# Two transformer layers on one core: layer 0's rows projected group by group, even token tiles first, norms on GpSimd, ternary steps moved

## The chip, the cores and the metric

The program runs on one core of one Trainium2 chip. The metric is the device time of one execution in microseconds (us); lower is better. The engines are called by the profile's names: PE (TensorE matmul), PEld (its weight loads), DVE (VectorE), ACT (ScalarE), POOL (GpSimd) and SP (SyncE, which here only issues DMAs).

## The reference

Two layers, each of which normalizes its input over the last axis and adds attention and a feed-forward block to it. x has 2 batches of 1024 tokens of 256 features. All arithmetic is float32 except where the weights are made ternary. Cut to layer 0, which the change touches:

```
xn = layernorm(x)
# attention, 16 heads of 16 features; the reshape takes a head out of the token axis
Q = (xn @ Wq.T).reshape(2, 16, 1024, 16)      # K and V alike
weights = softmax(causal(Q K^T) / sqrt(16))
x1 = x + (weights V) @ Wp.T + bp
# feed-forward with ternary weights, one scale for each 64 weights
h  = relu(xn @ ternary(W_fc).T) ** 2
x1 = x1 + rms_norm(h) @ ternary(W_proj).T
```

The reshape (1024 tokens of 256 features into 16 heads of 1024 positions of 16 features) gives head h the tokens 64h to 64h+63, and each of these tokens gives 16 positions. Layer 1 is a latent attention with 16 heads and a gated feed-forward block with ternary weights; the change leaves its code as it is.

## The kernel before

**Tiles.** x lies in SBUF as x_sb, 16 tiles of 128 tokens, 8 for each batch (E = 256, SC = 512, S = 1024, KC = 2). `ln_stats` takes means and variances of tiles on DVE and a square root on ACT, `ln_rstd` the reciprocal on DVE, `ln_norm` normalizes two tiles into one buffer xn (there is one such buffer), and `ln_turn` transposes these on PE and copies them with ACT into xnT, which holds the normalized tokens of a batch with the features on the partitions.

**Projections.** `project(b, i, m, k)` makes half m of the features of q, k or v (i = 0, 1, 2) for half k of batch b: two matmuls with 512 moving columns. The profile's L228 shows each float32 matmul as two records. When both halves k are there, L246 stores 128 rows of 1024 tokens to DRAM (rows), in an SP DMA. `fetch(g, i)` reads group g's rows back with four SP DMAs (L256), so that the 16 features of a head lie on partitions; group g = 4b + h4 has the four heads h4, h4+4, h4+8, h4+12 of its batch, that is, 64 tokens of each 256. `permute(g, i)` reorders the fetched rows into head tiles (DVE for group 0's k, ACT for group 0's q and group 1's k, else POOL). k and v share one staging buffer.

**The order.** All engines run an order written out by hand (`manual_schedule`). Ahead of the loop stand a prologue (tiles 0 to 7 normalized and turned, k and q of batch 0 projected in full, group 0's k and q fetched and permuted, tiles 8 to 11 turned, one ternary step), and then a loop over groups g = -1 to 8 with 12 steps n each. In a step of group g the row maxima of group g+1 are made (`maxima`: matmuls L307, reductions on DVE L318 and L323), the scores and weights of group g (`scores`: L348, the exponential on ACT at L355, the causal cut on POOL at L358), the product with v of two steps earlier (`product`), and one piece of `fill`, the queue of PE work: the 12 projections of batch 1 first (all in group 0), then layer 0's feed-forward (L430 and L461), from group 1 on. Group -1 has only group 0's maxima, and beside them v of batch 0, the last tiles' norms and turns, and group 1's fetches and permutes.

In group -1 the maxima go through two PSUM pairs (`ps_pair`): a step's first pair waits until DVE has reduced the step before's first pair. From group 0 on they use `ps_bank`, three banks shared with projections, transposes and the feed-forward.

**Ternary steps.** Eight blocks of the feed-forward's weights are made ternary by `ternary`: begin (two ACT passes, L197 and L199), scale (one matmul, L203), pick (five DVE passes, L207 to L215, then two POOL passes, L216 and L217). One stands in the prologue, four in group -1 (n = 2, 3, 10, 11) and three in group 0 (n = 2, 3, 10).

**Buffers.** The projections' SBUF results are in the tag "four" (4 buffers). The tag "temp" (6 buffers, given out in turn) holds the discarded output of the L318 reductions (junk), q_th of the ternary steps and the feed-forward's relu and sq.

Of the kernel before, what the change touches and what calls it, by code (L numbers as in the profile page):

```python
# [17 lines left out]
F32 = mybir.dt.float32  # L18
BF16 = mybir.dt.bfloat16
AF = mybir.ActivationFunctionType  # L20
ALU = mybir.AluOpType
# [25 lines left out]
def two_layers(ctx: ExitStack, tc: tile.TileContext, a: dict, out: bass.AP):  # L47
# [13 lines left out]
    for g in range(4):  # L61
        nc.sync.dma_start(x_sb[:, 4 * g : 4 * g + 4, :], x_d[:, 4 * g : 4 * g + 4, :])
# [41 lines left out]
    with ExitStack() as scope:  # L104
# [48 lines left out]
        def ln_stats(g):  # L153
            for n in range(4 * g, 4 * g + 4):
                st = small.tile([P, 6], F32, tag="ln_st", name="ln_st")
                nc.vector.bn_stats(st, x_sb[:, n, :])
                nc.vector.bn_aggr(mv[:, n, :], st)
            r = rstd[:, 4 * g : 4 * g + 4]
            nc.scalar.activation(r, mv[:, 4 * g : 4 * g + 4, 1], AF.Sqrt, bias=eps["ln"])

        def ln_rstd(g):
            r = rstd[:, 4 * g : 4 * g + 4]
            nc.vector.reciprocal(r, r)

        def ln_norm(n):

            xn = l0t.tile([P, SC], F32, tag="xn", name="xn", bufs=1)
            for k in range(2):
                nc.vector.tensor_scalar(
                    xn[:, k * E : (k + 1) * E], x_sb[:, n + k, :], mv[:, n + k, 0:1],  # L170
                    rstd[:, n + k : n + k + 1], ALU.subtract, ALU.mult,
                )
            return xn

        def ln_turn(xnT, n, xn=None):

            xn = ln_norm(n) if xn is None else xn
            pt = ps_bank()
            for k in range(2):
                for kc in range(KC):  # L180
                    nc.tensor.transpose(
                        pt[:, (2 * kc + k) * P : (2 * kc + k + 1) * P],
                        xn[:, k * E + kc * P : k * E + (kc + 1) * P], ident,
                    )
            at = (n % TB) * P
            nc.scalar.copy(
                xnT[n // TB][:, :, at : at + 2 * P], pt.rearrange("p (c t) -> p c t", c=KC)
            )
# [33 lines left out]
        rows, pend = {}, {}  # L222

        def project(b, i, m, k):

            pw = ps_bank()
            for kc in range(KC):
                nc.tensor.matmul(  # L228
                    pw, wqkv[:, i, kc, m * P : (m + 1) * P],
                    xnT[b][:, kc, k * SC : (k + 1) * SC], start=(kc == 0), stop=(kc == KC - 1),  # L230
                )
            if (b, i, m) not in pend:
                pend[b, i, m] = l0t.tile([P, S], F32, tag="four", name=f"proj{i}_{b}_{m}", bufs=4)
            half = pend[b, i, m][:, k * SC : (k + 1) * SC]
            if b or m:
                nc.scalar.activation(half, pw, AF.Copy, scale=0.25 if i == 0 else 1.0)
            elif i == 0:
                nc.vector.tensor_scalar(half, pw, 0.25, None, ALU.mult)
            else:
                nc.vector.tensor_copy(half, pw)  # L240
            if k == 0:
                return
            proj = pend.pop((b, i, m))
            if m == 0:
                rows[b, i] = dram.tile([2 * P, S], F32, tag=f"rows{b}{i}", name=f"rows{b}{i}")
            nc.sync.dma_start(rows[b, i][m * P : (m + 1) * P, :], proj)  # L246
# [3 lines left out]
        def fetch(g, i):  # L250

            b, h4 = divmod(g, 4)
            src = rows[b, i].rearrange("(j d) t -> d j t", d=D0)
            for c in range(4):
                at = 256 * c + GC * h4
                nc.sync.dma_start(stage[i][32 * c : 32 * c + D0], src[:, :, at : at + GC])  # L256
# [163 lines left out]
        def ffn(n):  # L420
# [56 lines left out]
        fill = [  # L477
            lambda i=i, m=m, k=k: project(1, i, m, k)
            for i in (1, 0, 2) for m in range(2) for k in range(2)
        ] + [x for n in range(B * S // SC) for x in ffn(n)]  # L480
# [236 lines left out]
        with tc.manual_schedule():  # L717

            ln_stats(0)
            ln_rstd(0)  # L720
            ln_turn(xnT, 0)
            ln_turn(xnT, 2)
            project(0, 1, 0, 0)
            project(0, 1, 1, 0)
            ln_stats(1)
            ln_rstd(1)
            ln_turn(xnT, 4)
            ln_turn(xnT, 6)
            for m in range(2):
                project(0, 1, m, 1)  # L730
            fetch(0, 1)
            for m in range(2):
                for k in range(2):
                    project(0, 0, m, k)
            fetch(0, 0)
            begin, scale, pick = weight_steps.pop(0)
            begin()
            ln_stats(2)
            ln_rstd(2)
            ln_turn(xnT, 8)  # L740
            ln_turn(xnT, 10)
            scale()
            permute(0, 1)
            permute(0, 0)
            pick()

            rest = None
            for g in range(-1, NG + 1):
                this, nxt = 0 <= g < NG, g + 1 < NG
                for n in range(12 if g < NG else 2):  # L750
# [4 lines left out]
                    if g < 1 and n in (2, 3, 10, 11) and weight_steps:  # L755
                        block = weight_steps.pop(0)
                        block[0]()
# [25 lines left out]
                    if g == -1:  # L783
                        if n < 2:
                            for k_ in range(2):
                                project(0, 2, n, k_)
                        if n == 1:
                            fetch(0, 2)
                            ln_stats(3)
                            ln_rstd(3)  # L790
                        if n in (4, 6):
                            ln_turn(xnT, 8 + n, xn)
                        if n in (3, 5):
                            xn = ln_norm(12 + n - 3)
                        if n == 4:
                            permute(0, 2)
                            fetch(1, 1)
                            fetch(1, 0)
                        if n in (7, 8):
                            permute(1, 8 - n)  # L800
# [38 lines left out]
                    if g == NG - 3:  # L839
                        if n < 2:  # L840
                            ln_stats(n)
                        if n == 3:
                            ln_rstd(0)
                            ln_rstd(1)
                            xnT1.append(main.tile([P, KC, S], F32, tag="xnT0", name="xnT1_0"))
                        if n in (5, 6, 7, 8):
                            ln_turn(xnT1, 2 * (n - 5), xn)
                        if n in (4, 5, 6, 7):
                            xn = ln_norm(2 * (n - 4))
# [15 lines left out]
            for i in range(TB):  # L865
# [9 lines left out]
                if i == 4:  # L875
                    ln_stats(2)
                if i == 5:
                    ln_rstd(2)
                    xnT1.append(main.tile([P, KC, S], F32, tag="xnT1", name="xnT1_1"))
                    xn = ln_norm(8)  # L880
# [6 lines left out]
            ln_stats(3)  # L887
            ln_rstd(3)
# [411 lines left out]
```

## Time and profile before

| | |
|---|---|
| median of 3 runs | 1390.37 us (1389.55 to 1397.06) |
| the profiled execution | 1391.99 us, span 1390.3 us |
| mean granted PE clock | 0.966 of full |
| PE busy | 1289.6 us (93%), 15614 matmul records |
| DVE, ACT, POOL busy | 765.3 us (55%), 674.3 us (49%), 459.7 us (33%) |
| L228 (projections) in the chain that ended last | 4% |

The chain that ended last is the work followed back from the last instruction to what released it; 81% of it is PE. In the timeline a line gives start, duration (of a merged run of instructions), engine, source line, operation, output<-input, shapes, count, and in brackets the idle time before it and what ended that. The windows of the trace give, for a stretch of time, the busy time of each engine with its count of instructions, then the granted PE clock (1.00 is full), the DMA share and the rate. SPq lines are DMA issues of the SP queue.

### The profile page before, as it was taken

The numbers are of one execution on the slowest core, as the hardware profiler recorded it, in microseconds if no ns is written. First come the engines' busy times: TensorE is split into PE (matmuls) and PEld (weight loads), VectorE is DVE, ScalarE is ACT, GpSimd is POOL, SyncE is SP. The second block draws the span as 40 slices with busy tenths as digits, with TensorE's granted clock in tenths as the row PEclk, the third lists the DMA queues.
The fourth block names the chain that finished last, engine by engine and source line by source line (L and its number), as shares of the span: only waits on it lengthen the run. The fifth ranks groups of instructions, "written<-read, shape, count | busy, mean of one in ns | idle before, by whom it ended". The sixth has DMA issues, their size and how long they took to land.

```text
span 1390.3 us, 36291 instructions
## 1 busy us (share of the span) xinstructions
PE 1289.6 (93%) x15614; PEld 775.9 (56%) x15614; DVE 765.3 (55%) x1909; ACT 674.3 (49%) x1250; POOL 459.7 (33%) x494
## 2 busy tenths in 40 slices
PE   5589999899999998999999789999999999999996
PEld 2233336345355363446577456777766667777665
DVE  3775544546455555313433666666666666666662
ACT  1224474453554744664331555555555555555541
POOL 2133242433422421110321444444444444444420
PEclk9759999989999999999999999999999999999999
DMA  5212120010001000000112400000000000000000
GB/s 190 79 23 69 57 58 16 9 16 8 16 8 16 8 24 0 19 16 1 57 57 85 83 6 18 9 26 7 25 10 25 10 18 17 15 21 10 17 7 21
DMA packets 61008, 41.09 MB, mean 30 GB/s; under 512 B 37648, under 2 KB 56848, under 8 KB 60592
## 3 DMA queue, kind: packets, MB, share of 16 engines
q1 hardware_dynamic: 60000, 35.51, 9.7%
q8 instruction: 122, 2.00, 0.6%
q0 software_dynamic: 416, 2.49, 0.4%
q10 hardware_dynamic: 432, 0.79, 0.2%
q14 instruction: 38, 0.31, 0.1%
HBM read 26.18 MB, written 10.49 MB: 26 GB/s over the span
## 4 chain that ended last, share of the span: by engine, by line
PE 81%; DVE 9%; issue 4%; ACT 4%; POOL 2%; DMA 1%; SPq 0%; DVEq 0%; ACTq 0%; POOLq 0%
PE ps_s L1061 15%; PE ps_m L307 11%; PE ps_o L1109 11%; PE ps_m L558 6%; PE ps_o L373 5%; PE ps_m L461 5%; PE ps_t L1001 4%; PE ps_m L430 4%; PE ps_m L228 4%; PE ps_m L573 3%; PE ps_t L1136 3%; PE ps_t L994 2%; DVE p L1068 2%; DVE pT L1078 1%; PE ps_s L307 1%
## 5 line engine op out<-in xcount | busy, mean ns | idle before, releaser
L1072 ACT ACTIVATE p<-p,nmax 128x1024 f32<-128x1024 f32 (+7 forms) x256 | 197.2, 771 | 209.7 <-DVE nmax L1068 208.9
L1061 PE MATMUL ps_s<-kT,qc 128*128 128x512 f32 (+3 forms) x768 | 279.2, 497 | 20.7 <-DVE nmax L1068 12.0
L1068 DVE CUSTOM_DVE_ANT_0 p<-ps_s,wpe 128x1024 f32<-128x1024 f32 (+7 forms) x256 | 184.8, 744 | 176.3 <-PE ps_s L1061 175.3
L355 ACT ACTIVATE p<-ps_s 128x1024 f32<-128x1024 f32 (+1 forms) x192 | 152.6, 808 | 165.1 <-PE ps_s L348 160.1
L307 PE MATMUL ps_m<-head,head 16*128 16x512 f32 (+3 forms) x672 | 192.5, 547 | 20.7 <-DVE nmx L318 14.0
L1061 PEld LDWEIGHTS ps_s<-kT,qc 128*128 128x128 f32 x768 | 130.6, 190 | 131.4 <-issue 93.5
L1078 DVE STREAM_TRANSPOSE pT<-p 128x1024 f32<-128x1024 f32 (+7 forms) x256 | 185.9, 758 | 22.1 <-ACT p L1072 21.0
L348 PE MATMUL ps_s<-head,head 17*128 17x512 f32 (+3 forms) x768 | 170.7, 549 | 0.0
L1109 PE MATMUL ps_o<-pT,vrep 32*64 32x128 f32 x9216 | 150.6, 273 | 9.8 <-issue 7.2
L1109 PEld LDWEIGHTS ps_o<-pT,vrep 32*64 32x64 f32 x9216 | 133.8, 130 | 37.8 <-issue 30.8
L1034 POOL TENSOR_TENSOR qc<-t,t 32x512 f32<-32x512 f32 x120 | 152.2, 1268 | 8.1
L307 PEld LDWEIGHTS ps_m<-head,head 16*128 16x128 f32 x672 | 71.3, 187 | 120.2 <-DVE nmx L318 37.1
L358 POOL TENSOR_SCALAR_AFFINE_SELECT p<-p 128x256 f32<-128x256 f32 x128 | 51.2, 406 | 240.5 <-ACT p L355 239.2
L1029 POOL TENSOR_TENSOR t<-t,cosq 128x512 f32<-128x512 f32 x28 | 35.7, 1273 | 258.9 <-issue 144.2
L323 DVE TENSOR_REDUCE nmx<-ps_m 128x1 f32<-128x512 f32 x112 | 72.2, 686 | 44.0 <-PE ps_s L348 35.3
L558 PE MATMUL ps_m<-xnT,w 128*128 128x512 f32 x192 | 94.4, 620 | 0.0
L318 DVE CUSTOM_DVE_ANT_0 junk<-ps_m,maskz,nmx 128x512 f32<-128x512 f32 (+3 forms) x112 | 57.7, 548 | 59.6 <-PE ps_s L348 45.1
L373 PE MATMUL ps_o<-p,v 128*32 128x512 f32 (+3 forms) x768 | 82.4, 502 | 0.0
L461 PEld LDWEIGHTS ps_m<-wpr,hT 128*128 128x128 f32 x512 | 61.2, 196 | 17.1 <-issue 6.6
L318 DVE CUSTOM_DVE_ANT_0 junk<-ps_m,maskz 128x512 f32<-128x512 f32 (+3 forms) x112 | 50.5, 487 | 34.3 <-PE ps_s L348 31.6
L461 PE MATMUL ps_m<-wpr,hT 128*128 128x128 f32 x512 | 67.4, 286 | 0.0
L430 PE MATMUL ps_m<-xnT,wfc 128*128 128x512 f32 x128 | 67.1, 649 | 0.2
(176 smaller groups left out, 1758.1 us busy)
## 6 DMA issues: line engine op xcount, KB each, us to landing
rows<-proj SPq DMA_DIRECT2D x12, 512.0 KB, 2.6
stage<-rows SPq DMA_DIRECT2D x96, 64.0 KB, 3.1
w<-in_w SPq DMA_DIRECT2D x3, 768.0 KB, 4.8
x_sb<-in_x SPq DMA_DIRECT2D x4, 512.0 KB, 12.2
x<-x_sb SPq DMA_DIRECT2D x4, 512.0 KB, 3.2
fold_wo<-in_wo SPq DMA_DIRECT2D x8, 256.0 KB, 3.3
vrep<-kv SPq DMA_DIRECT2D x32, 64.0 KB, 2.2
xin<-x SPq DMA_DIRECT2D x16, 128.0 KB, 2.2
```

Of the source, the lines that this page charges most:

```text
L307: nc.tensor.matmul(t[:, :w], quad(q, c, D0)[:, i * P : (i + 1) * P], quad(k, c, D0)[:, k0 : k0 + w], start=True, stop=True, tile_position= ...
L348: nc.tensor.matmul(t[:, c % 2, :w], quad(k, c, D0 + 1)[:, j * P : (j + 1) * P], quad(q, c, D0 + 1)[:, at : at + w], start=True, stop=True, ...
L355: nc.scalar.activation(p[:, pair[0] : pair[0] + 2, :w], t[:, :, :w], AF.Exp)
L373: nc.tensor.matmul(quad(box["o"], c)[:, SC - w :], values[g][:, j, 32 * c : 32 * c + 32], p[:, c, :w], start=(j == 0), stop=(j == 4 * iq + ...
L461: nc.tensor.matmul(po[:, :P], f["h", hc // 2][:, hc % 2, t * P : (t + 1) * P], wpr[:, hc, cols], start=(hc == 0), stop=(hc == NH0 - 1),)
L558: nc.tensor.matmul(pw, w1t[f"w{i + 1}"][:, kc, hc * P : (hc + 1) * P], xnT1[n // 2][:, kc, (n % 2) * SC : (n % 2 + 1) * SC], start=(kc == ...
L1034: (even, odd)[x].tensor_tensor(self.qc[64 + 32 * x : 96 + 32 * x, hh], t1[at : at + 32], t2[at : at + 32], ALU.add,)
L1061: nc.tensor.matmul(sc[:, j * SC + n0 : j * SC + n1], s.q[k].qc[:, h // QP, h % QP, :], kT[:, s.b * S + n0 : s.b * S + n1], start=True, sto ...
L1068: nc.vector.tensor_tensor_reduce(p, sc[:, j * SC : j * SC + w], maskw[:, S - w :], -1.0, 3.0e38, ALU.add, ALU.min, nmax,)
L1072: nc.scalar.activation(p, p, AF.Exp, bias=nmax, scale=-1.0, accum_out=s.rsum[:, k, h : h + 1])
L1078: nc.vector.transpose(s.pT[:, at, h, :], s.p[k, h])
L1109: nc.tensor.matmul(s.o[64 * hh : 64 * hh + 64, c, k * P : (k + 1) * P], vrep[32 * c : 32 * c + 32, s.b * 32 + sb, :], s.pT[32 * c : 32 * c ...
```

## The change

- `project(g, i)` now makes one group's rows: 4 matmuls of 256 moving columns (both halves m of the features; the moving columns are four pieces of 64 tokens), one evacuation of 128x512 (on DVE for k and v of group 0 and v of group 1, else on ACT) into a "temp" buffer, and one store of 256 KB. There are 24 such calls, where there were 24 of two matmuls with a store for each second one.
- x is loaded, and the statistics and the turns are done, by even and odd tiles of each batch. Groups 0 and 1 need the even tiles of batch 0 alone, groups 2 and 3 its odd ones.
- The prologue projects q, k and v of groups 0 and 1 from the even tiles; it takes the statistics of all 16 tiles; it normalizes the odd tiles of batch 0 on POOL.
- Groups 2 and 3 are projected in group -1 (n = 1, 2, 3, 5, 6, 9), and batch 1's tiles are normalized there, on POOL, and turned.
- The eight ternary steps stand in group -1 (n = 8, 10), group 0 (n = 2, 3, 10, 11) and group 1 (n = 2, 3).
- `fill` begins with the 12 calls for groups 4 to 7.

```
-    for g in range(4):
-        nc.sync.dma_start(x_sb[:, 4 * g : 4 * g + 4, :], x_d[:, 4 * g : 4 * g + 4, :])
+    EVEN_ODD = [slice(b * TB + k, (b + 1) * TB, 2) for b in range(B) for k in range(2)]
+    for at in EVEN_ODD:
+        nc.sync.dma_start(x_sb[:, at, :], x_d[:, at, :])
...
-        def project(b, i, m, k):
+        def project(g, i, engine=nc.scalar):
+            b, h4 = divmod(g, 4)
             pw = ps_bank()
+            for m in range(2):
+                for kc in range(KC):
+                    nc.tensor.matmul(
+                        pw[:, m * E : (m + 1) * E], wqkv[:, i, kc, m * P : (m + 1) * P],
+                        xnT[b][:, kc, :].rearrange("p (c h t) -> p c h t", c=4, h=4)[:, :, h4, :],
+                        start=(kc == 0), stop=(kc == KC - 1),
+                    )
+            proj = temp("proj")
...
+            rows[g, i] = dram.tile([2 * P, E], F32, tag=f"rows{g}{i}", name=f"rows{g}{i}")
+            nc.sync.dma_start(
+                rows[g, i].rearrange("(m p) t -> p m t", p=P), proj.rearrange("p (m t) -> p m t", m=2)
+            )
...
+            even, odd, even1, odd1 = EVEN_ODD
+            ln_stats(even)
+            ln_rstd(even)
+            for n in (0, 4):
+                ln_turn(xnT, n, ln_norm(n, 2), 2)
+            project(0, 1, nc.vector)
+            fetch(0, 1)
+            project(0, 0)
+            fetch(0, 0)
+            ln_stats(odd)
+            project(0, 2, nc.vector)
+            project(1, 1)
+            ln_stats(even1)
+            ln_stats(odd1)
+            for at in (odd, even1, odd1):
+                ln_rstd(at)
+            project(1, 0)
+            project(1, 2, nc.vector)
+            for n in (1, 5):
+                ln_turn(xnT, n, ln_norm(n, 2, nc.gpsimd), 2)
+            permute(0, 1)
+            permute(0, 0)
+
+            first = {
+                0: [lambda: turns.append(ln_norm(8, 2, nc.gpsimd))],
+                1: [lambda: fetch(0, 2), lambda: project(2, 1)],
+                2: [lambda: ln_turn(xnT, 8, turns.pop(), 2), lambda: project(2, 0),
+                    lambda: turns.append(ln_norm(12, 2, nc.gpsimd))],
+                3: [lambda: project(2, 2)],
+                4: [lambda: permute(0, 2), lambda: fetch(1, 1), lambda: fetch(1, 0),
+                    lambda: ln_turn(xnT, 12, turns.pop(), 2)],
+                5: [lambda: project(3, 1), lambda: turns.append(ln_norm(9, 2, nc.gpsimd))],
+                6: [lambda: project(3, 0)],
+                7: [lambda: permute(1, 1), lambda: ln_turn(xnT, 9, turns.pop(), 2),
+                    lambda: turns.append(ln_norm(13, 2, nc.gpsimd))],
+                8: [lambda: permute(1, 0)],
+                9: [lambda: project(3, 2), lambda: ln_turn(xnT, 13, turns.pop(), 2)],
+            }
+            turns = []
+            ternary_at = {(-1, 8), (-1, 10), (0, 2), (0, 3), (0, 10), (0, 11), (1, 2), (1, 3)}
...
-                    if g < 1 and n in (2, 3, 10, 11) and weight_steps:
+                    if (g, n) in ternary_at:
```

## The prediction

> **What bounds the kernel now.** I read the page's 40 slices first (34.8 us each; busy tenths), then the start's timeline.
>
> ```profile
> PE   5589999899999998999999789999999999999996
> DVE  3775544546455555313433666666666666666662
> PEclk9759999989999999999999999999999999999999
> ```
>
> From slice 3 on PE is at nine tenths and full clock: time saved ahead of it should last to the end, and PE work or stalls added after it add time. Only the first 100 us have something to give. First the way to the first maximum, SP's queue and then PE and ACT:
>
> ```profile
> 28.07 1.96 SPq L246 DMA_DIRECT2D rows<-proj  x2
> 32.37 1.80 SPq L256 DMA_DIRECT2D stage<-rows  x4
> 34.26 2.63 SPq L246 DMA_DIRECT2D rows<-proj  x2
> 39.24 1.79 SPq L256 DMA_DIRECT2D stage<-rows  x4
> ```
> ```profile
> 13.78 5.12 PE L228 MATMUL ps_m<-xnT,wqkv 128*128 128x512 f32 x8 [0.68 <-ACT xnT L186]
> 43.69 1.95 ACT L265 COPY head<-stage 128x1024 f32<-128x1024 f32 x1 [2.57 <-DMA stage<-rows]
> 45.69 2.09 PE L307 MATMUL ps_s<-head,head 16*128 16x512 f32 x8 [4.97 <-ACT head L265]
> ```
>
> PE is ready to project at 13.8, but k's stores leave at 28, q's fetch at 39, and group -1 starts at 45.7. Then the windows over group -1 (busy time of PE, PEld, DVE, ACT, POOL; clock; DMA):
>
> ```profile
> 50.00:60.00 10.00, 9.00 (x37) 3.46 (x35) 7.52 (x30) 2.47 (x5) 0.00 (x0) 0.96 0.24 99
> 60.00:70.00 10.00, 4.58 (x19) 2.07 (x21) 9.65 (x23) 1.85 (x3) 3.84 (x4) 0.55 0.13 34
> 70.00:80.00 10.00, 9.80 (x32) 3.88 (x32) 7.22 (x13) 2.40 (x2) 3.07 (x2) 0.50 0.35 52
> 90.00:100.00 10.00, 7.86 (x30) 3.14 (x28) 9.22 (x29) 4.15 (x5) 2.53 (x2) 0.50 0.00 1
> ```
>
> DVE leads, behind it PE at half clock, each waiting for the other. PE finds group 0's first banks at 95.8, but DVE reduces into group 0 only after a ternary block:
>
> ```profile
> 96.26 0.68 DVE L207 TENSOR_SCALAR q_sc<-ps_m 128x512 bf16<-128x512 f32 x1
> 99.32 0.69 DVE L215 TENSOR_TENSOR q_th<-q_th,q_sg 128x512 f32<-128x512 f32 x1
> 99.93 0.68 DVE L318 CUSTOM_DVE_ANT_0 junk<-ps_m,maskz 128x512 f32<-128x512 f32 x1
> ```
>
> This hand-over, 99.93, is what I move.
>
> **Part 1, the way to the first maximum: -11.3.** Load, statistics, table load and two turns are as before: PE projects at 13.8. k of group 0 is 8 records of 256 columns; at half clock 512 took 0.86, so 8 x 0.43 = 3.4: 17.2. DVE evacuates in 0.69: stored at 17.9. A store was followed by its fetch 2.7 later (second store 29.7, fetch 32.4), four issues take 1.8: q's store goes out at 22.4 behind them, q's fetch at 25.1, and its data are there 4.45 later (39.24 to 43.69), at 29.6. But q's permute is queued on ACT behind the copies of the odd turns. Their norms, now on POOL, need reciprocals that stand on DVE behind three sets of statistics (2.2 each) and an evacuation: 17.9 + 6.6 + 0.7 + 0.9 (waiting for PE) = 26.2. POOL's pair of 256-column norms is not in the trace; the nearest rows:
>
> ```profile
> L544 POOL TENSOR_SCALAR neg<-w,th 128x512 f32<-128x512 f32 x9 | 13.9, 1560 | 28.6 <-DVE th L540 17.2 <-PE ps_m L307 11.5
> L622 POOL TENSOR_SCALAR qa<-qa,ssq 128x192 f32<-128x192 f32 x16 | 12.4, 791 | 75.6 <-DVE ssq L619 75.6
> ```
>
> Between them 256 columns make 0.94, a pair 1.9 (bounds 0.72, L806's 256-column add, and 1.56: start 33.5 or 36.9). 26.2 + 1.9 + 0.8 (transposes), then, as there is one xn, again 1.9 + 0.8, ACT 0.6: 32.4. Permute 1.95: 34.4 instead of 45.7.
>
> The Trainium skill's "GPSIMD Engine Reference" (4.1 Engine selection) calls one-input elementwise work on GpSimd roughly line-rate, which at DVE's 0.41 would start group -1 about 2 earlier; the rows above, twice DVE's, speak against it.
>
> **Part 2, group -1: -8.9.** DVE loses two ternary blocks (2.92 each), statistics (2.4), norms (0.73 + 2.08) and two evacuations (1.4): 12.4; it keeps 24.2 of reductions, one 0.69 and two blocks, 30.7. PE gains two projections and two turns: six projections of 1.86 at full clock (part 4) or 3.42 at half. I walked the steps. Maxima start at 34.4 at half clock, and as before (45.69 to 50.46) n=0 is reduced 4.8 later, its first pair 3.5 later, at 37.9. Then n=1's two pairs (384 columns, 2.3 at half clock) and its projection (3.42) end at 43.5. After it n=2 and n=3 are short (256 and 128 columns) and each followed by a projection, so PE is dense and full clock comes: done at 46.7 and 49.0; n=4 (two pairs 1.1, a turn 0.6) at 50.7. n=5's pairs wait for DVE (four reductions of 0.62 a step, from 49.9); if the clock has fallen again they take 3.3 and the projection 3.42: 57.9. n=6 ends at 62.4, n=7 at 64.1. DVE reduces n=8 by 68.6, its block ends at 71.5; n=9's projection and turn hold PE until 74.2, so n=10 is reduced by 76.7, its block ends at 79.6, and n=11 takes 1.1: hand-over 80.7. With full clock throughout it is 77.1, with half clock throughout 92.4. I take 79.7, near the mixed case, because L228 went to full clock each time it ran dense for some 3.3 (17.0, 27.2, 51.1, 105.9). Parts 1 and 2: 99.9 - 79.7 = 20.2.
>
> The window 70 to 80 has PE busy 9.80 of 10 at 0.50: L307's 16-row tiles did not raise the clock. "TensorE: Matmul & The Clock Gate" (Part 1) of the Trainium skill says one busy window of about 3.4 us releases it; by that alone the hand-over would be 77.1, a sum 2.6 lower.
>
> **Part 3, three ternary steps that move behind the hand-over: +6.5.** One more block in group 0 (n=11), two in group 1. What one did in group 0, n=2:
>
> ```profile
> 117.98 0.69 DVE L215 TENSOR_TENSOR q_th<-q_th,q_sg 128x512 f32<-128x512 f32 x1
> 118.94 0.47 PE L307 MATMUL ps_m<-head,head 16*128 16x128 f32 x1 [1.15 <-DVE nmx L318]
> 119.58 3.41 PE L228 MATMUL ps_m<-xnT,wqkv 128*128 128x512 f32 x4
> ```
>
> DVE's block keeps the next reductions back, so PE lacks banks: 1.15 idle, 0.2 more, then L228 at half clock (3.41 for 1.98): 2.8. At n=10 it was 0.9. I take 1.5 in group 0 and 2.5 each in group 1, where POOL idles 5.1 between 180 and 192 and gets 5.06 more (behind it: the causal cuts, acc's adds and group 3's permutes). Bounds: 0 (DVE is busy only half the time there; a gain is excluded, as work is only added) to 3 x 2.8 = 8.4.
>
> **Part 4, narrower matmuls: +1.6.** L1136 has 256 columns: 16 records in 3.71 in the chain, 0.232 each, against 0.427 for 512. A projection is 8 x 0.232 = 1.86 for 4 x 0.427 = 1.71; 12 in group 0, some waiting for DVE anyway. Reading the moving columns in four pieces is in no row: from nothing to L461's 128-column pitch (67.4 / 512 = 0.13), +4.7 in all.
>
> **At nothing.** x by even and odd tiles: same pieces; loads land by 17.5 and are needed at 23.9. Twelve more stores on SP, 0.4 each: SP then mostly waits. fetch(1,1) waits on SP for POOL's permute of v, about 49, and behind it stands group 3's first store, ready at 55.8; were that permute 7 later, the store, and with it a "temp" buffer, would be late. A "temp" buffer with a projection comes up again six allocations later, a full step, for a store of 2.6. POOL's norms run beside reductions that POOL work left at 2.48 per four. A pair of DVE norms took 2.08 instead of 0.73 beside POOL's L216 (at 63.5); so POOL's norms may hold DVE's permute of k back by a norm pair, 1.9, and q's permute, the later one, still hides that.
>
> **Sum.** -20.2 + 6.5 + 1.6 = -12.1: an execution like the profiled one, 1391.99, would take 1379.9. The median is 1.6 below it: 1378.3.
>
> **Rivals.** (a) Full clock throughout and cheap blocks: -22.8 + 2.7 + 0.9 = -19.2, 1371. For: six dense projections; against: n=4, n=7 and n=8 have none. (b) Half clock throughout group -1: hand-over 92.4, -7.5 + 8.1 = +0.6, 1391. For: clock 0.50 to 0.55 from 60 to 100; against: L228 always warmed. (c) Slower: each moved block costs what a POOL and DVE chain cost at L544 (PE idle 6.1 from 273 to 279, then the clock at half until 286: 9.5): 28.5 + 1.6 - 20.2 = +9.9, 1400; it decides from 6.2 a block. For: POOL is full there; against: what POOL gives in these blocks, no maximum waits for.
>
> **Numbers.** About 0.5% (7 us) is what a measurement can tell. Forecast case 0.55, (a) 0.20, (b) 0.17, (c) 0.08. Faster: 0.55 + 0.20 + 0.03 of (b) = 0.78; same 0.14; slower 0.08. The range runs from (a) with its bounds, 1368, to the middle of (b), 1391, leaving out half of (b), (c) and a little below.
>
> **What would show it.** First L307 at 34 (33 to 37); clock near 1.0 at 44 to 50; hand-over at 77 to 81; no PE gap over 3 around the blocks of groups 0 and 1; from group 2 on the same durations as before. A first maximum after 40, or clock 0.5 at 44 to 70, would prove parts 1 or 2 wrong.

## The result and the profile after

The changed kernel takes 1395.72 us (median of 20 runs; 1395.49 in a second comparison), the kernel before 1393.26 beside it. The ratio is 1.0005, interval 0.9986 to 1.0023: no difference that can be measured. The prediction was 1378.3, with a range of 1368 to 1391: it is 17 too low, and the time lies outside the range. Two of the 20 runs were far slower (1519.61 and 6802.62 us), the first profiled execution among them, at 0.82 of the clock; the profile shown here is that of a second execution, span 1393.7, time 1395.43.

The page's slices:

```profile
PE   4889999898999998999999799999999999999996
DVE  3655555546455546213433666666666675666662
PEclk9778989999999999999999899999999999999999
```

PE is at eight tenths in the second slice (35 to 70 us), where it was at five. But the clock is at eight in the fourth and the sixth slice (105 to 139 and 174 to 209), where it was at nine. The way to the first maximum (SP's queue, then POOL, ACT and PE in the timeline):

```profile
18.12 0.37 SPq L243 DMA_DIRECT2D rows<-proj  x1
20.34 1.81 SPq L253 DMA_DIRECT2D stage<-rows  x4
22.25 0.39 SPq L243 DMA_DIRECT2D rows<-proj  x1
25.17 1.78 SPq L253 DMA_DIRECT2D stage<-rows  x4
```
```profile
30.16 2.43 POOL L173 TENSOR_SCALAR xn<-x_sb,ln_mv,ln_rstd 128x256 f32<-128x256 f32 x2 [0.67 <-PE ps_m L184]
33.85 1.93 ACT L262 COPY head<-stage 128x1024 f32<-128x1024 f32 x1
35.83 2.09 PE L304 MATMUL ps_s<-head,head 16*128 16x512 f32 x8 [2.50 <-ACT head L262]
```

k's store leaves at 18.1 and q's fetch at 25.2 (predicted 17.9 and 25.1). The first maximum starts at 35.8 instead of 45.7. The hand-over:

```profile
80.09 0.69 DVE L217 TENSOR_TENSOR q_th<-q_th,q_sg 128x512 f32<-128x512 f32 x1
81.79 0.68 DVE L315 CUSTOM_DVE_ANT_0 junk<-ps_m,maskz 128x512 f32<-128x512 f32 x1
```

DVE reduces into group 0 at 81.8 instead of 99.9: 18.1 are won. They are gone 170 us later, but for 1.9. The clearest place is group 1, from its first fill step to its eighth (the windows' columns are busy PE, PEld, DVE, ACT, POOL, then clock, DMA share and rate), first in the kernel before and then in the changed one:

```profile
169.80:204.60 34.80, 34.80 (x216) 13.83 (x213) 17.30 (x48) 24.42 (x36) 15.77 (x18) 1.00 0.26 69
```
```profile
159.70:205.90 46.20, 41.84 (x217) 16.10 (x214) 24.45 (x58) 26.68 (x40) 24.79 (x24) 0.85 0.22 52
```

Before, PE is busy for all of 34.8 us at full clock. After, the stretch takes 46.2: PE is idle for 46.2 - 41.8 = 4.4, and a clock of 0.85 costs 46.2 x 0.15 = 6.9. What is left, 34.9, is the work of before. The two ternary blocks that now stand at n = 2 and 3 do it; the first of them in the timeline:

```profile
173.19 1.50 POOL L441 TENSOR_TENSOR acc<-acc,sq 128x512 f32<-128x512 f32 x1 [2.66 <-ACT sq L440]
173.61 1.64 DVE L217 TENSOR_TENSOR q_th<-q_th,q_sg 128x512 f32<-128x512 f32 x1
...
175.17 0.24 DVE L387 RECIPROCAL rinv<-ps_m 128x16 f32<-128x16 f32 x1
175.45 0.42 DVE L389 TENSOR_TENSOR ctx_n<-ps_m,rinv 128x256 f32<-128x256 f32 x1
176.02 0.69 PE L304 MATMUL ps_m<-head,head 16*128 16x128 f32 x2 [2.70 <-DVE ctx_n L389]
176.87 3.78 PE L427 MATMUL ps_m<-xnT,wfc 128*128 128x512 f32 x4
...
185.72 1.22 PE L304 MATMUL ps_m<-head,head 16*128 16x512 f32 x1 [1.57 <-DVE nmx L320]
187.74 2.93 PE L427 MATMUL ps_m<-xnT,wfc 128*128 128x512 f32 x3
```

DVE's fifth pass takes 1.64 beside POOL's sum of the feed-forward; in the blocks of groups -1 and 0 it takes 0.69. Behind it on DVE stand the normalization of the context (L387, L389) and then n=3's reductions; PE waits until the normalization has freed a bank, 2.70. Then the up projection takes 3.78 instead of 1.98: half clock, from 174.6 to 181.4. The second block brings a pause of 1.57 and half clock of its own, from 184.9 to 191.7.

All this can be summed for every kernel below. "Hand-over" is DVE's first reduction with maskz that reads ps_m. "Group 0" is the time from its first fill step (the projection at n=0) to group 1's; "group 1" from its first fill step to its eighth. The last column is when group 2's fifth fill step starts, the first up projection of the second of the feed-forward's four pieces. Times in us, from one profiled execution each.

| kernel | hand-over | group 0 | group 1 | group 2's fifth step |
|---|---|---|---|---|
| before | 99.9 | 67.1 | 34.8 | 251.3 |
| changed (e1) | 81.8 | 74.6 | 46.2 | 249.4 |
| e2, three early | 93.2 | 75.5 | 34.8 | 252.9 |
| e3, three left out | 87.4 | 72.5 | 34.8 | 241.5 |
| e4, other buffers | 84.7 | 74.6 | 46.2 | 252.3 |
| e5, spaced | 82.4 | 75.2 | 48.9 | 253.2 |
| e6, all late | 81.8 | 78.2 | 48.4 | 254.8 |
| e7, adjacent | 85.3 | 81.4 | 45.4 | 258.8 |
| e8, no POOL passes in the last three | 85.2 | 74.6 | 46.2 | 252.9 |
| e10, wide matmuls | 84.3 | 76.0 | 47.7 | 254.8 |
| e11, before, two late | 96.7 | 67.0 | 45.3 | 255.3 |
| e9, two in prologue | 90.1 | 74.6 | 34.8 | 246.3 |
| e12 | 86.1 | 78.5 | 48.9 | 262.9 |
| e13 | 88.8 | 78.5 | 37.1 | 250.6 |
| e14, one in prologue | 87.9 | 78.5 | 37.0 | 249.7 |
| e15, pass on POOL, group 1 | 84.1 | 76.1 | 41.7 | 248.7 |
| e16, pass on POOL, late six | 85.2 | 69.3 | 44.7 | 246.0 |
| e17, e9 with the pass on POOL | 89.8 | 69.3 | 36.4 | 242.2 |
| e18, all on POOL | 89.9 | 69.7 | 36.5 | 242.9 |

Between group 1's eighth step and that point, 46.6 to 46.7 us pass in the profiles of before, e2 and e12 and 43.5 in the others: 3.2 at the clock. From there to the end of the program the code is the same in all, and it takes 1139.0 us in the profile of before, 1144.3 in e1's and up to 1146.3 (e15). e1's 5.3 more lie in layer 1: from the last matmul of layer 0's output projection to the end before takes 724.3 at a clock of 1.00 and e1 729.6 at 0.98, and all 19 profiles 723 to 730. What sets the clock there was not followed, so the time of a single profile can't decide about a few us.

### The profile page after: what moved, and what is told of

It reads as the page before. It is cut to its first block, busy times and chain, and to the rows that moved or that the text cites. A ratio compares the mean times of both kernels' runs of the same rounds, so it can differ in the third digit from the quotient of the medians.

```text
span 1517.9 us, 36532 instructions
## 1 busy us (share of the span) xinstructions
PE 1442.4 (95%) x15710; PEld 858.5 (57%) x15710; DVE 763.9 (50%) x1894; ACT 677.0 (45%) x1253; POOL 475.0 (31%) x506
## 4 chain that ended last, share of the span: by engine, by line
PE 87%; DVE 5%; issue 2%; ACT 1%; POOL 1%; DVEq 0%; POOLq 0%; ACTq 0%
PE ps_s L1055 17%; PE ps_m L304 11%; PE ps_o L1103 10%; PE ps_m L554 7%; PE ps_m L427 5%; PE ps_o L370 5%; PE ps_m L458 5%; PE ps_t L995 5%; PE ps_t L1130 4%; PE ps_m L569 3%; PE ps_m L231 3%; PE ps_t L988 3%; DVE p L1062 1%; PE ps_m L592 1%; PE ps_s L345 1%
## 5 line engine op out<-in xcount | busy, mean ns | idle before, releaser
L1055 PE MATMUL ps_s<-kT,qc 128*128 128x512 f32 (+3 forms) x768 | 315.6, 555 | 11.9 <-DVE nmax L1062 9.0
L304 PE MATMUL ps_m<-head,head 16*128 16x512 f32 (+3 forms) x672 | 208.4, 598 | 21.2 <-DVE nmx L315 12.1
L345 PE MATMUL ps_s<-head,head 17*128 17x512 f32 (+3 forms) x768 | 188.3, 604 | 1.9 <-DVE nmx L315 1.9
L1103 PE MATMUL ps_o<-pT,vrep 32*64 32x128 f32 x9216 | 164.1, 292 | 6.8 <-issue 4.2
L1103 PEld LDWEIGHTS ps_o<-pT,vrep 32*64 32x64 f32 x9216 | 146.6, 133 | 39.7 <-issue 31.7
L554 PE MATMUL ps_m<-xnT,w 128*128 128x512 f32 x192 | 108.6, 701 | 0.0
L370 PE MATMUL ps_o<-p,v 128*32 128x512 f32 (+3 forms) x768 | 89.8, 544 | 0.0
L427 PE MATMUL ps_m<-xnT,wfc 128*128 128x512 f32 x128 | 81.1, 768 | 0.0
L458 PE MATMUL ps_m<-wpr,hT 128*128 128x128 f32 x512 | 75.1, 305 | 0.0
L1130 PE MATMUL ps_t<-wvo,xT 128*128 128x256 f32 x256 | 71.6, 431 | 3.0 <-DVE xT L1113 1.8
```

The lines of the kernel that those rows point to most:

```text
L304: nc.tensor.matmul(t[:, :w], quad(q, c, D0)[:, i * P : (i + 1) * P], quad(k, c, D0)[:, k0 : k0 + w], start=True, stop=True, tile_position= ...
L345: nc.tensor.matmul(t[:, c % 2, :w], quad(k, c, D0 + 1)[:, j * P : (j + 1) * P], quad(q, c, D0 + 1)[:, at : at + w], start=True, stop=True, ...
L370: nc.tensor.matmul(quad(box["o"], c)[:, SC - w :], values[g][:, j, 32 * c : 32 * c + 32], p[:, c, :w], start=(j == 0), stop=(j == 4 * iq + ...
L427: nc.tensor.matmul(ph, wfc[:, kc, hc * P : (hc + 1) * P], xnT[n // 2][:, kc, (n % 2) * SC : (n % 2 + 1) * SC], start=(kc == 0), stop=(kc = ...
L458: nc.tensor.matmul(po[:, :P], f["h", hc // 2][:, hc % 2, t * P : (t + 1) * P], wpr[:, hc, cols], start=(hc == 0), stop=(hc == NH0 - 1),)
L554: nc.tensor.matmul(pw, w1t[f"w{i + 1}"][:, kc, hc * P : (hc + 1) * P], xnT1[n // 2][:, kc, (n % 2) * SC : (n % 2 + 1) * SC], start=(kc == ...
```

## The experiments

Medians are in us, beside those of the kernel before on the same chip; in brackets stand the ratio to it and its 95% interval. The letters of the theories belong to each expectation, with the words beside them.

**The changed kernel again, with the ternary blocks moved back, left out, and with other buffers.** Four kernels in one comparison. e1 is the changed kernel; the others have these edits:

```
e2: ternary_at = {(-1, 2), (-1, 3), (-1, 8), (-1, 10), (-1, 11), (0, 2), (0, 3), (0, 10)}
e3: ternary_at = {(-1, 8), (-1, 10), (0, 2), (0, 3), (0, 10)}     # five blocks
e4: -            proj = temp("proj")
    +            proj = l0t.tile([P, S], F32, tag="four", name="proj", bufs=4)[:, :SC]
```

> The changed kernel as it is, for a second profile at full granted clock. All theories: about 0 to 0.3% from the kernel before. Theory A (the hand-over is early, the three late ternary blocks give it back): DVE's first reduction into group 0 at 80 to 84 (99.9 before), the first bp add of group 0 some 15 before that of the kernel before, the first bp add of group 1 within 5 of it, with PE gaps and half-clock L427 matmuls around the blocks of group 1. Theory B (the projections of group 0 give it back, by their pieces or by the shared temp buffers): group 0's steps are longer than before already at its first two steps. Theory C (given back later): group 2 and 3 still start 12 or more earlier than before and the lead goes after that.

> The changed kernel with the three late ternary blocks moved forward: steps in group -1 at n = 2, 3, 8, 10, 11 and in group 0 at n = 2, 3, 10, none in group 1. Theory A: hand-over later by 4 to 9 (DVE work of three blocks, 8.8), but no stall in group 1: faster than the changed kernel by 5 to 12 us. Theory B and C: no faster than the changed kernel (within 3 us), or slower by the later hand-over.

> The changed kernel without its last three ternary blocks (group 0 n = 11, group 1 n = 2 and 3 are left out, so three blocks of the projection weights of the feed-forward are not made ternary). Theory A: faster than the changed kernel by 12 to 18 us, which is what three blocks at 4 to 6 each cost. My predicted price of 6.5 for the three: faster by 6.5. Theory B and C: faster by less than 5.

> The changed kernel with the projections' results in the four buffers that they had before (tag four) instead of the six temp buffers shared with junk and q_th. Theory B (buffers): faster than the changed kernel by 5 us or more. Theory A and C: within 3 us of it.

Measured: e1 1395.49 (1.0004, 0.9980 to 1.0028), e2 1400.14 (1.0027, 1.0000 to 1.0054), e3 1382.65 (0.9915, 0.9885 to 0.9946), e4 1396.06 (1.0004, 0.9978 to 1.0029); before 1393.84. Without its last three blocks the changed kernel is 12.8 faster, 4.3 a block; my price was 6.5 for all three. But in group -1 they are hardly cheaper: in e2 the hand-over is at 93.2, 11.4 later than in e1 and 8.5 later than the median of the kernels with the same code up to there (84.7, below), some 3 a block, and group 0 does not become shorter. The expectation that early blocks would give a faster kernel failed. e1's profile fits theory A. The shared buffers cost nothing.

**One part undone, and that part alone.** e10 makes batch 1's projections in group 0 as before, with 512 columns; e11 is the kernel before with two blocks moved from group -1 to group 1.

```
e10: fill = [lambda i=i, m=m, k=k: project_wide(1, i, m, k)
             for i in (1, 0, 2) for m in range(2) for k in range(2)] + ...
     # project_wide is project of the kernel before; fetch of groups 4 to 7 reads its rows
e11: -  if g < 1 and n in (2, 3, 10, 11) and weight_steps:
     +  if (g, n) in {(-1, 10), (-1, 11), (0, 2), (0, 3), (0, 10), (1, 2), (1, 3)}:
```

> The changed kernel with one part undone: batch 1's projections in group 0 are made as in the kernel before, 512 contiguous moving columns, their results in the buffers of the hidden rows and six stores of 512 KB. With the same three blocks of group 0 the kernel before loses 3.4 us to the clock between group 0's and group 1's first fill steps, a variant of the changed kernel 8.7. Theory B (the narrow matmuls and their pieces of 64 columns let the clock fall, or cost 1.6 to 4.7 as the prediction had it): 3 to 6 us faster than the changed kernel, 1389 to 1392, and 3 to 4 us at the clock in group 0. Theory A (blocks alone): no difference, 1394 to 1397.

> The kernel before with two of its ternary blocks moved from group -1 (n = 2 and 3) to group 1 (n = 2 and 3), and nothing else. Theory A: the hand-over, 99.93 in the kernel before, comes 5 to 7 us earlier, and group 1 loses some 11 us (idle PE 4.4, clock 6.9), as in the changed kernel: slower than the kernel before by 3 to 7, 1396 to 1400. By the prediction's price (2.5 us a block) it would be 1 to 2 us faster, 1390 to 1392.

Measured: e10 1395.90 (1.0003, 0.9983 to 1.0024), e11 1401.83 (1.0045, 1.0017 to 1.0074); before 1394.80. The narrow matmuls cost nothing that shows, and group 0 is as long with wide ones (76.0). e11 is the clean test of the late blocks. Its hand-over is 3.2 earlier than before's:

```profile
96.74 0.68 DVE L318 CUSTOM_DVE_ANT_0 junk<-ps_m,maskz 128x512 f32<-128x512 f32 x1
```

Its first maximum comes 2.6 later, at 48.3 for 45.7, with the same code up to there; from it to the hand-over are 48.4 us for 54.2, some 2.9 less for each block taken out. Group 0 is as long as before's, group 1 takes 45.3 for 34.8, and the time is 6 us longer. So two blocks in group 1 cost 10.5 in this kernel and 11.4 in the changed one, where I had 5.0:

```profile
166.50:211.80 45.30, 41.09 (x217) 15.79 (x214) 24.81 (x58) 26.71 (x40) 21.73 (x22) 0.89 0.21 53
```

It is much the same as after: 4.2 idle and 5.0 at the clock, in a kernel without any other part of the change.

**Which of the block's engines, and which places.** In e5, e6 and e7 only the set of places differs; e8 leaves POOL's passes out of the last three blocks.

```
e5: ternary_at = {(-1, 8), (-1, 10), (0, 3), (0, 5), (0, 7), (0, 11), (1, 3), (1, 5)}
e6: ternary_at = {(0, 1), (0, 3), (0, 5), (0, 7), (0, 9), (0, 11), (1, 3), (1, 5)}
e7: ternary_at = {(-1, 8), (-1, 10), (0, 3), (0, 4), (0, 6), (0, 7), (1, 3), (1, 4)}
e8: +  if add:                       # add = (g, n) < (0, 11)
           nc.gpsimd.tensor_tensor(th, th, w, ALU.subtract)
           nc.gpsimd.tensor_tensor(w, w, th, ALU.add)
```

> The eight ternary blocks in the same numbers as in the changed kernel (two in group -1, four in group 0, two in group 1), but no two in neighbouring steps, and each late one ahead of a step with 512-column maxima (n = 3, 5, 7, 11 of group 0, n = 3, 5 of group 1). Theory A (what costs is that a block holds DVE back while PE has only a narrow step's work left, 2.70 us of idle PE after group 1's n=2, and that the clock then stays at half for 7 to 15 us, in which the next block hits again): no L427 or L231 of 3.8 us after group 0's n=0, no idle stretch of PE over 1.6 us at a block, the blocks cost 1 to 2 us each, and the time is 1381 to 1387. Theory B (a block costs its 3 us of DVE and 2.5 us of POOL wherever it stands behind the hand-over): as the changed kernel, 1393 to 1398.

> As the spaced kernel, but the two blocks of group -1 are moved behind the hand-over too: n = 1, 3, 5, 7, 9, 11 of group 0 and n = 3, 5 of group 1. Theory A: group -1 loses two blocks of 2.9 us on DVE, so the hand-over comes 4 to 6 earlier than in the spaced kernel, and the two cost 1 to 2 each behind it: 1 to 3 us faster than the spaced kernel, 1378 to 1385. Theory B: the two cost about 4 each there, as the three late blocks did (12.8 us in all): no faster than the spaced kernel, 1393 to 1399. A third outcome, the dense blocks in group 0 (every second step) bring half clock of their own: slower than the spaced kernel by 3 to 8.

> The same numbers of blocks in each group as in the changed kernel, in neighbouring steps, but each ahead of a step with 512-column maxima (n = 3, 4, 6, 7 of group 0, n = 3, 4 of group 1). It tells what of theory A matters. If it is the narrow step behind a block (n = 3 has 128 columns): as the spaced kernel, 1381 to 1387. If it is that two blocks follow each other within 5 us: as the changed kernel, 1393 to 1398, with half clock after the second of each pair. Theory B: 1393 to 1398 too, without half clock.

> The changed kernel with GpSimd's two passes (subtract and add) left out of the last three ternary blocks (group 0's n=11, group 1's n=2 and 3), so that those weights stay as they were; ACT, PE and the five DVE passes of these blocks stay. Theory A (DVE's hold on the reductions costs): no more than 2 us faster than the changed kernel, 1393 to 1396, with PE idle 2 to 3 us behind group 1's n=2 as before and half clock after it. Theory B's other half (POOL, which gets 5 us more work between group 1's n=2 and n=4, holds back the causal cuts and the feed-forward's sums): 6 to 12 us faster, 1383 to 1389.

Measured: e5 1396.04 (1.0021, 1.0003 to 1.0038), e6 1405.01 (1.0080, 1.0050 to 1.0111), e7 1404.63 (1.0089, 1.0062 to 1.0115), e8 1395.84 (1.0008, 0.9984 to 1.0031); before 1392.76. e8 fits theory A: POOL's two passes do not matter; PE waits 2.71 for the same context normalization without them. But theory A's part about places failed: spacing the blocks and setting them ahead of wide steps does not help. In e5 PE's pauses are shorter (1.2 us in group 0, for 3.3 in e1) and the clock still costs 10.3 there (8.9 in e1). e6 has no block at all in group -1, and its hand-over is still at 81.8: without them PE sets the pace there, at a granted clock of 0.62 to 0.86 from 40 to 80. I found no cheap place for a block of five DVE passes in groups 0 and 1, and neighbouring ones ahead of wide steps (e7) are dearest, 81.4 in group 0.

**DVE's hold, one pass shorter.** A block's hold is the time for which its passes keep DVE from the reductions. In e15 POOL makes the fifth pass in group 1's two blocks, in e16 in all six blocks behind the hand-over.

```
-                nc.vector.tensor_tensor(th, th, t["sg"], ALU.mult)
+                engine.tensor_tensor(th, th, t["sg"], ALU.mult)
...
-                        block[2]()
+                        block[2](nc.gpsimd if g == 1 else nc.vector)     # e15; e16: g >= 0
```

> The changed kernel with the last of DVE's five passes (q_th by q_sg) made on GpSimd in group 1's two ternary blocks. That pass took 1.64 us beside GpSimd's sum of the feed-forward (1.50 us) where it takes 0.69 in groups -1 and 0, so DVE's hold falls from some 3.9 to 2.2 us and GpSimd gets 1.3 more a block. Theory A (DVE's hold sets the idle PE, and that the half clock): PE's 2.70 us idle behind group 1's n=2 falls to 0.5 to 1.3, group 1's first eight fill steps from 46.2 to 37 to 42 us, and the time by 4 to 9, 1387 to 1392. Theory B (GpSimd's extra work holds the causal cuts and sums back): no gain, 1394 to 1399.

> The same in all six blocks behind the hand-over, so in group 0's four too, where the pass took 0.69. Theory A: PE's pause behind group 0's n=2 (1.16 us) falls by some 0.7; if that keeps the clock up, group 0 shortens from 74.6 to 66 to 70 us and the time to 1380 to 1388; if not, as the kernel with group 1's two alone. Theory B: no gain, 1394 to 1400.

Measured: e15 1395.10 (0.9995, 0.9970 to 1.0020), e16 1388.80 (0.9964, 0.9946 to 0.9982); before 1392.58. In e15 the pause behind group 1's n=2 falls from 2.70 to 1.03, as expected, and group 1 from 46.2 to 41.7, although POOL has more to do:

```profile
179.52 0.49 PE L304 MATMUL ps_m<-head,head 16*128 16x128 f32 x2 [1.03 <-DVE ctx_n L389]
...
179.83 1.15 POOL L217 TENSOR_TENSOR q_th<-q_th,q_sg 128x512 f32<-128x512 f32 x1
180.06 3.64 PE L427 MATMUL ps_m<-xnT,wfc 128*128 128x512 f32 x4
```

One stretch of half clock is left (3.64), and the median did not move, so the expected 4 to 9 failed: this profile's hand-over and group 0 are together 3.8 later than e1's, and the interval of the ratio would still hold a gain of 4. In e16 group 1 falls only to 44.7, but group 0 from 74.6 to 69.3, and there the median moves, 6.7 below the changed kernel's:

```profile
104.65 0.37 PE L304 MATMUL ps_m<-head,head 16*128 16x128 f32 x1 [0.43 <-DVE nmx L315]
...
105.08 1.99 PE L231 MATMUL ps_m<-xnT,wqkv 128*128 128x256 f32 x8
```

The pause behind group 0's n=2 is 0.43 instead of 1.15 and the projection after it runs at full clock.

**Blocks where DVE is free.** e9 puts group 1's two blocks into the prologue, e14 one there and one at n=11 of group -1. e12 and e13 test whether the blocks' places at the end of group -1 set the clock in group 0.

```
e9:  +  block[0]()
     +  xn = ln_norm(1, 2, nc.gpsimd)
     +  block[1]()
        permute(0, 1)
     +  ln_turn(xnT, 1, xn, 2)
     +  xn = ln_norm(5, 2, nc.gpsimd)
     +  block[2]()
     +  # the next block: begin, scale; ln_turn(xnT, 5, xn, 2); pick
        permute(0, 0)
     ternary_at = {(-1, 8), (-1, 10), (0, 2), (0, 3), (0, 10), (0, 11)}
e12: (-1, 10), (-1, 11) in the changed kernel's set, for (-1, 8), (-1, 10)
e13: e9 with e12's places
e14: one block in the prologue, and
     {(-1, 8), (-1, 10), (-1, 11), (0, 2), (0, 3), (0, 10), (0, 11)}
```

> The two ternary blocks of group 1 stand in the prologue instead, where DVE has nothing to do from 28 to 36 us; the other six stay where the changed kernel has them. Theory A (a late block costs idle PE and half clock behind the hand-over, an early one only DVE's time, which is free here): group 1's losses of 4.4 us of idle PE and 6.9 us at the clock go; the first maximum may come 0 to 3 later (POOL's passes beside its norms), so 8 to 11 us faster than the changed kernel: 1384 to 1388. Theory C (the gain of an early hand-over is given back later whatever comes between): no faster than 1392.

> The changed kernel with the two blocks of group -1 at its last two steps (n = 10 and 11, where the kernel before has two of its four) instead of n = 8 and 10. The same three blocks in group 0 cost 67.1 us of group 0 in the kernel before and 72.6 in the changed one without its last three blocks: 5.5 more, nearly all at the clock. Theory D (what stands at the hand-over decides when the clock comes back in group 0, and by that where its half-clock stretches fall): group 0 shortens by 4 to 6 us from its 74.6, and the time by 2 to 5, 1390 to 1393, if the hand-over is not more than 2 later. Theory E (it does not depend on the hand-over): group 0 stays at 74 to 76 and the time at 1394 to 1398.

> Both: group 1's two blocks in the prologue, and group -1's two at its last steps. The prologue kernel was 5.4 us faster than the changed kernel, and lost 8 us of hand-over (90.1 for 81.8) to half clock in group -1. Theory D: faster than the prologue kernel by 3 to 6 us, 1384 to 1387. Theory E: as the prologue kernel, 1388 to 1392.

> One of group 1's two blocks in the prologue, the other at n = 11 of group -1 (blocks there: 8, 10, 11). With one block the first maximum should stay at 36 to 37; group -1 pays 3 to 4 us for the third block; group 1's 11.3 us of idle PE and half clock go. Theory A: 5 to 8 us faster than the changed kernel, 1387 to 1390. If the prologue's blocks and the third in group -1 let the clock fall through group -1, as in the prologue kernel (hand-over at 90): 1390 to 1394.

Measured: e9 1390.10 (0.9967, 0.9948 to 0.9986; before 1394.80), e12 1405.13 (1.0063, 1.0039 to 1.0086), e13 1393.23 (0.9989, 0.9968 to 1.0009), e14 1393.12 (0.9996, 0.9974 to 1.0019; before 1392.68). e9 takes group 1's loss away altogether:

```profile
168.00:202.80 34.80, 34.80 (x215) 13.84 (x212) 17.07 (x48) 24.42 (x36) 18.91 (x20) 1.00 0.29 69
```

It is only 5.4 faster than the changed kernel because its hand-over is at 90.1: group -1 starts 1.6 later and then has half clock through 40 to 50 and 60 to 70. So it stays above the expected 1384 to 1388. Theory D of e12 fell: with blocks at the end of group -1 group 0 is longer, 78.5. e13 and e14, which have a block at n=11 of group -1 too, have that group 0 as well, and hand-overs of 88.8 and 87.9: no gain.

**The version that the runs point to.** e17 is e9 with the fifth pass on POOL in group 0's four blocks; e18 has it in group -1's two as well.

> The prologue kernel (group 1's two blocks ahead of the first maximum) with the last DVE pass of group 0's four blocks made on GpSimd. The first alone was 5.4 us faster than the changed kernel, the second (in group 0) shortened that group from 74.6 to 69.3. Theory A, by which both take away idle PE and half clock at different places: their gains add, group 0 at 68 to 71 and group 1's first eight fill steps at 34.8, 1382 to 1387, faster than both kernels. If the clock in group 0 depends on more than that pause: as the prologue kernel, 1388 to 1392.

> As the kernel with both, and the same pass on GpSimd in group -1's two blocks too. DVE leads there, so two passes of 0.69 should bring the hand-over 1 to 1.5 earlier if GpSimd, which also makes batch 1's norms there, does not hold a turn back: 0 to 2 faster than the kernel with both, 1380 to 1387. If GpSimd's work delays a turn or a permute in group -1: 1 to 4 slower than it.

Measured: e17 1384.05 (0.9921, 0.9889 to 0.9952), e18 1387.54 (0.9933, 0.9906 to 0.9961); before 1392.86. e17 is faster than both kernels, by some 9 us than the one before and by 11 than the changed one. The gains of e9 and e16 add: group 0 is 69.3 as in e16, and group 1 has no pause (its 36.4 is 34.8 and half clock at its start). The same pass on POOL in group -1 gave nothing that shows (hand-over 89.95 for 89.78).

## Why the prediction was wrong, step by step

**Part 1 was right.** First maximum 35.8 for 34.4 (33 to 37 was the test). What was off is POOL's pair of norms: 2.43, where I took 1.9 from two rows on either side. (The terms as written add up to 34.1, not 34.4; it changes nothing.) The Trainium skill's "GPSIMD Engine Reference" (4.1 Engine selection), by which the pair would take about DVE's time, is further off: 1.21 each on GpSimd against DVE's 0.41 here.

**Part 2 took the lucky end.** The hand-over was 81.8 in the profile of the changed kernel, for 79.7, and n=2 and n=3 ran at full clock as I had walked them. But the code up to there is the same in e1, e3, e5, e7, e8, e10, e15 and e16, and their hand-overs lie between 81.8 and 87.4, median 84.7. From 45 to 55 us the granted clock is 1.00 in e1 and between 0.66 and 0.91 in e3, e8, e10, e15 and e16. So the lead is 15 rather than 20: half clock there is more common than I allowed. The kernel before has one profile only, so its own 99.9 may be off by some us too: e11's first maximum comes 2.6 later with the same code.

**Part 3 is the step that failed.** I priced a moved block by one that lay in group 0 of the kernel before, 1.5 and 2.5, and took a bound of 2.8. The three cost 2.1 (e1's group 0 against e3's) and 11.4 together (group 1), 13.5 for my 6.5; e3's time gives 12.8. Three things were missing. In group 1 the feed-forward runs, so POOL's sums stand beside DVE's passes and stretch one of them by 0.95, and in the first block the context's normalization stands behind it; in group 0 neither is there. PE, not DVE, sets the pace, and a pause of PE costs itself and then the clock: 6.9 of the 11.4. And both blocks did so, each with its own pause and its own half clock. I had written that DVE is busy only half the time there, and had weighed POOL as the risk (its idle time from 180 to 192 is 4.6, not 5.1); e8 shows that POOL's two added passes are free (group 1 takes 46.2 without them too), and the groups of e15 and e16 that DVE's length is not. Rival (c) had the mechanism, PE idle and then half clock, at 9.5 a block, deciding from 6.2. In group 1 it is 5.7 a block, so the moved blocks alone did not decide. With the 5.5 that group 0 lost besides, which e3 has without them (below), 19.0 are lost behind the hand-over, and that is where the gain is used up.

**Part 4 cost nothing.** Projections in fill start 1.92 apart from what follows them where the wide ones took 1.91, the step lengths in group 0 without blocks are the same to 0.05, and e10 gives no difference.

**What was in no step: group 0's own 5.5.** With the same three blocks at the same places group 0 takes 67.1 in the kernel before and 72.5 in e3, and the difference is at the clock (half clock costs 3.1 and 8.9). It is not the narrow matmuls (e10), the buffers (e4), the number of blocks (e3), nor their places in group -1 (e12). PE's pauses are nearly the same: behind n=10 it is 0.90 in both, but the projection behind it takes 1.98 in the kernel before and in e11, 3.3 to 3.8 in the changed kernel, e3, e9 and e10. The traces show what differs. The clock changes only at the ends of windows of 3.41 us, and the clock comes back 2.7 us after group 0's first projection starts in the kernel before and in e11, 3.8 to 4.7 after it in the others; from there to the end of that pause it is 59.0 in the kernel before against 61.4 in e1 and e3. So the same pause falls differently into the windows. Here are the window with the pause and the next one, with the busy time of the projection alone (PE, PEld, then clock, DMA share and rate), in the kernel before and then in e3:

```profile
163.45:166.86 3.41, 1.98 (x4) 0.68 (x4) 1.00 0.00 0
166.87:170.28 3.41, 0.00 (x0) 0.00 (x0) 1.00 0.37 154
```
```profile
152.95:156.35 3.40, 0.00 (x0) 0.00 (x0) 1.00 0.22 77
156.37:159.77 3.40, 2.76 (x7) 2.22 (x8) 0.50 0.00 0
```

PE is busy for 2.52 and 2.47 us in the two windows with the pause. In the kernel before a whole projection stands in that window and the clock stays; in e3 the projection comes in the next one, which runs at half. The pause behind n=3 does the same: 0.48 in a window with 1.34 us of projection leaves the clock at full in the kernel before, 0.68 in a window without any brings two windows of half clock in e3. No run moved the windows alone, so this is read from the traces and not shown by an experiment. A shorter hold makes most of it go (69.3 in e16, e17).

**The sum, in e1's profile against before's:** hand-over -18.1, group 0 +8.1 (with 0.5 ahead of its first projection), group 1 +11.4, the clock behind group 1's eighth step -3.2: -1.9 in group 2, for -12.1 predicted. With the median hand-over it is +1, which fits the times. The spans of the two profiles differ by 3.4; the other 5.3 are layer 1's clock, which was in no step either.

## What to carry over

A step that is moved off one engine's critical stretch should be priced where it lands: read there what runs beside it on the other engines, what stands behind it on its queue, and whether PE, which sets the pace there, is made to pause. Where PE is dense, a pause costs itself and the half clock that may follow; in group 1 that was more than the pauses (6.9 for 4.4 in the changed kernel, 5.0 for 4.2 in e11). The same 0.90 of pause cost the clock in e3 and not in the kernel before, by what else stood in its window. Moving work to where its engine has nothing to do (e9), or making the hold shorter (e16), paid; spreading the same holds (e5, e6, e7) did not.

## What the runs showed of the hardware

- Half clock comes in steps. In windows of 10 us of the changed kernel the clock is again and again 1.00, 0.83 or 0.67, which is 0, 3.4 or 6.6 us at half:

```profile
110.00:120.00 10.00, 10.00 (x43) 4.96 (x44) 4.13 (x7) 3.53 (x4) 4.26 (x4) 0.67 0.07 26
150.00:160.00 10.00, 8.90 (x40) 4.63 (x41) 6.36 (x21) 3.37 (x7) 5.11 (x6) 0.83 0.08 26
```

"TensorE: Matmul & The Clock Gate" (Part 1) of the Trainium skill gives a window of about 3.4 us for the release; the rows agree with that length, and show it for the way down too: in all 19 profiles every stretch of half clock is a whole number of 3.41 us.
- What else stands in the window of a pause tells whether the pause costs the clock. Between 95 and 250 us the 19 profiles have 74 windows at full clock with over 0.35 us of idle PE; in none of them is PE idle for the whole window (2.36 at most). 61 of them hold at most 0.84 us of projections, feed-forward matmuls and transposes (all on 128 rows), and half clock followed each; 13 hold 1.20 us or more, and it followed none, also not the two with a pause of 0.90. Of 646 windows with less idle time, 13 were followed by half clock.
- The same DVE pass of 128x512 takes 0.69 alone and 1.64 beside a GpSimd sum (itself 1.50 for 1.27), in both kernels' group 1 (e1 and e11).
- A block of 2.9 us of DVE work costs some 3 us where DVE leads (e2, three in group -1; e11, two taken out of it) and 4.3 behind the hand-over (e3), although DVE is busy only half the time there.
